# Moving the loads of the later layers' weights behind the first layer of the first group

## The chip, the core and the metric

The kernel runs on one core of a Trainium2 chip. The metric is the device time of one execution, in microseconds (us). A core has five engines with a queue of instructions each, worked off in order: TensorE (PE), VectorE (DVE), ScalarE (ACT), GpSimd (POOL) and SyncE (SP). Transfers are issued from the queues of SP, ACT and POOL; the issuing instruction stands in its queue like any other.

## What is computed

Four graph layers in a row, on 32 entries of 512 nodes with 256 features (float32), with one 512 x 512 matrix `adj` that is nearly all zeros: about eight entries a row besides the diagonal. Layers 0 and 3 are the same function with weights of their own (cut to what matters):

```python
pre_u = einsum('bud,dk->buk', h, W1[:d]);  pre_v = einsum('bvd,dk->bvk', h, W1[d:])
hidden = relu(pre_u[:, :, None, :] + pre_v[:, None, :, :] + b1)
S = sigmoid(einsum('buvk,ko->buvo', hidden, W2)[..., 0] + b2[0])
a = einsum('buv,bud->bvd', S * A, h)
m = einsum('uv,bud->bvd', A, h) * h
z = beta1 * h + beta2 * (a @ Wa + ba) + beta3 * (m @ Wm + bm)
```

Layer 1 is `z + relu((adj @ z) @ W.T + b)`, layer 2 an attention over all nodes with `W1`, `W2`, `b2`, `bias2` and `adj` added to the logits.

## The kernel before, in words

S is needed only where `adj` is not zero. The kernel counts the entries of a row first (class `Counts`) and branches: with few of them it takes `sparse_path`, which is what runs here. (`dense_path` is built as well and is not executed.)

**Tiles and groups.** The 32 entries are worked off in eight groups of four (`NB = 4`). For a group and a layer of the first kind there are these stages:

- `first`: the four entries are loaded (line 830, tile `h`), turned on PE (line 585), copied to `hT` by ACT (line 588) and put back to memory as `xT` (line 589). `pre` multiplies them with `W1` (line 601): the u half gets its bias on DVE (line 610) and is put into a table in memory (line 611, SP), the v half is copied by ACT (line 613, tile `v`) and put too (line 614, SP). DVE adds both for the diagonal (line 616) and sums them with `W2` (line 618). For each entry this is done in two halves of the nodes, so that a group has eight u and eight v puts. This needs of the weights only `W1`, `b1`, `W2` and `b2`.
- `edges`: 36 items of 128 table rows each are gathered (line 662, POOL, tile `rows`), the row of the other node is added (line 747, DVE; tile `mine`, loaded at line 708 by SP or gathered), and ReLU, `W2` and a sum follow (lines 755, 763 on DVE, line 733 on ACT). The results are put into a dense matrix in memory (line 655, POOL, `cells`). A gather may read any row, so the first one waits for all sixteen table puts.
- `middle`: the dense S is loaded back (line 791), and the rest of layer 0, layers 1 and 2 and the first stage of layer 3 follow, mostly on PE. Here `Wa`, `Wm` and the weights of layers 1 and 2 are used for the first time; for the first group `middle_before` makes some of it ahead.
- then `edges` again for layer 3, and `last`.

**The start.** Before all this, `Edges.build` makes the lists of the non-zero entries out of `adj`: four pieces that turn `adj` (lines 297 to 305), four that count along the rows and put `lists` into memory (lines 315 and 316), then for each eight positions a masked sum on DVE (line 359) and a Sign with a sum on ACT (line 370), and four gathers of `lists` (line 349, POOL). `zeros` writes zeros over the cells in memory, eight transfers of 512 KB from POOL (line 566).

**The other weights.** `Model.rest` is a generator with six pieces of code between its yields. Its first piece issues all loads of the weights that the first stage does not use: `gnn_loads` for layers 0 and 3 (three `beta`, line 84; `Wa` and `Wm`, line 120; `ba` and `bm` spread over the partitions, line 124: these on ACT's queue; `ba` and `bm` as columns, line 95, on SP's) and `others_loads` for layers 1 and 2 (`b2`, line 84, and the two weights at lines 147 and 148 on ACT; three columns on SP). That makes 17 loads on ACT and 7 on SP. The later pieces scale them by the betas on DVE (lines 131 to 138) and turn the weights of layers 1 and 2 on PE (line 160), copied by DVE (line 161). `ba`, `bm` and the two weights land in one buffer named `big` (2048 columns); the others have places of their own.

**What sets the order.** `sparse_path` gives each of these generators a list of times in units of a group, one per piece, and `weave` calls the pieces in the order of those times. That is the order in which the program is written down; a scheduling layer then places the instructions on the engines, and may move one ahead of others of its engine where nothing that it needs forbids that. In the built program all transfers that SP and ACT issue take one of eight semaphores in turn, and each waits until the last transfer on its semaphore has landed. The times that matter here: `setup` from -0.40 to -0.295, the `first` of group 0 from -0.385 to -0.30, `setup_behind` (the rest of `Edges.build`) from -0.285, `setup_rest` (the rest of `Model.rest`) from -0.26 to -0.20, and the edges of group 0 from -0.292.

Of the kernel before, what the change touches and what calls it, by code (L numbers as in the profile page):

```python
# [425 lines left out]
class Sparse:  # L426
# [110 lines left out]
    def setup(self):  # L537


        for w in (self.m.g0, self.m.g3):  # L540
            self.nc.vector.tensor_scalar(w["nb2"], w["b2"], -1.0, None, ALU.mult)
        self.zero = self.act.tile([P, GROUP], F32, name="zero", tag="hWa3")
        self.nc.gpsimd.memset(self.zero, 0.0)

        edges = self.built = self.e.build(self.counts, self.adjT, self.lists, self.psum, self.big, self.act)
        for _ in range(NC):
            next(edges)
            yield
        self.rest = self.m.rest(self.big(F32, 2048), self.psum)
        next(self.rest)  # L550
        self.zeros("0")
        yield
        for _ in range(NC + 2 * (OWN // 2 + 1)):
            next(edges)
            yield
# [609 lines left out]
def even(n):  # L1165
    return [1.0] * n
# [7 lines left out]
def spread(shares, a, b):  # L1174

    times, at = [], 0.0
    for share in shares:
        times.append(a + (b - a) * at / sum(shares))
        at += share
    return times  # L1180


def edge_times(ahead, a, b, behind, lead=LEAD):

    step = (b - a) / ITEMS
    first = [ahead + j * min(step, (a - ahead) / lead) for j in range(lead)]
    return first + spread(even(ITEMS), a, b) + spread(even(TAIL), b, behind)


def middle_shares(given):  # L1190


    hWa = [] if given else [1.7, 1.7]
    shares = list(hWa)
    for b in range(NB):
        more = hWa if b < NB - 1 else []
        shares += [] if given else [2.8, 2.8]
        shares += [3.4, 3.4, 1.0, 2.7]
        shares += [1.7, 3.4, 2.8, 4.5] + [0.9] * NC
        shares += [0.4, 0.4, 0.4, 1.0, 0.4, 1.0] + more + [1.5, 1.5]  # L1200
        shares += [2.8, 4.5] + [0.4] * NC + [0.5, 0.5]
    return shares + [0.1]


@with_exitstack
def sparse_path(ctx, m, counts, xr, outr, B):


    sp = Sparse(ctx, m, counts, xr, outr, B)
    last = B // NB - 1  # L1210
    streams = [
        (sp.setup(), spread(even(NC + 1 + NC + 2 * (OWN // 2 + 1) + 1), -0.40, -0.295), ""),
        (sp.setup_behind(), spread(even(2 * (OWN // 2 + 1) + 2 * PANELS + 4), -0.285, -0.16), ""),
        (sp.setup_rest(), spread(even(7), -0.26, -0.20), ""),
        (sp.zeros_behind(), spread(even(2), 0.15, 0.2), ""),
    ]
    for t in range(last + 1):
        g0, g3 = Group(sp, m.g0, f"0_{t}"), Group(sp, m.g3, f"3_{t}")
        start, end = (max(0.0, k - 0.47) for k in (t, t + 1))

        if t == 0:
            first = spread(FIRST, -0.385, -0.30)
            edges0 = edge_times(-0.292, -0.27, -0.03, -0.02, LEAD_AT_ENDS)
        elif t == 1:
            first = spread(FIRST, -0.28, -0.06)
            edges0 = edge_times(0.02, 0.07, start - 0.06, start - 0.04)
        else:
            first = spread(FIRST, start - 0.82, start - 0.56)
            if t > 2:
                first = [start - 1.25, start - 1.2] + spread(FIRST[2:], start - 1.14, start - 0.86)  # L1230
            edges0 = edge_times(start - 0.552, start - 0.505, start - 0.06, start - 0.04)
        edges3 = edge_times(end + 0.003, end + 0.05, end + 0.48, end + 0.54)
        parts = [(0, NB, end + 0.53, end + 0.56, end + 1.16)]
        if t + 3 <= last:
            parts = [(0, 2, end + 0.53, end + 0.56, end + 0.84), (2, NB, end + 1.06, end + 1.16, end + 1.46)]
        if t == last - 1:
            edges3 = edge_times(end + 0.003, end + 0.05, end + 0.46, end + 0.5)
            parts = [(0, NB, end + 0.67, end + 0.7, end + 1.06)]
        if t == last:
            end -= 0.2  # L1240
            edges3 = edge_times(end + 0.003, end + 0.02, end + 0.45, end + 0.46, LEAD_AT_ENDS)
            behind = end + 0.28, end + 0.4
        streams += [
            (sp.first(g0, t * NB), first, FIRST_US),
            (sp.edges(g0, ("yT", "mhT0", "hWa0") if t == 0 else ()), edges0, "free" if t > 2 else ""),
            (sp.middle(g0, g3, t * NB), spread(middle_shares(t == 0), start, end), "main"),
            (
                sp.edges(g3, *((("yT", "h1", "hT1"), ("mhT0", "hWa0")) if t == last else ())),
                edges3,
                "free",  # L1250
            ),
        ]
        if t == 0:
            streams.append((sp.middle_before(g0, 0), spread(AHEAD, -0.15, -0.03), ""))
        if t < last:
            for lo, hi, ahead, a, b in parts:
                times = [ahead] + spread(even((hi - lo) * 8 + 1), a, b)
                streams.append((sp.last(g3, t * NB, lo, hi), times, [0.0] + LAST_US * NB))
        else:
            streams.append((sp.last_before(g3, t * NB), spread(ENDS, *behind), ""))  # L1260
            streams.append((sp.last_half(g3), [end + 0.385] + spread(HALF_END, end + 0.42, end + 0.47), "free"))
            streams.append((sp.last_behind(g3, t * NB), spread(BEHIND, end + 0.5, end + 0.6), ""))
    sp.weave(streams)
# [191 lines left out]
@with_exitstack  # L1455
def adj_seq_kernel(ctx: ExitStack, tc: tile.TileContext, a: dict, out: bass.AP):
    nc = tc.nc
    x = a["x"]
    B = x.shape[0]
    xr = x.rearrange("b (c p) d -> b p c d", p=P)  # L1460
    outr = out.rearrange("b (c p) d -> b p c d", p=P)
    m = Model(ctx, tc, a)
    counts = Counts(ctx, m)
    excess = nc.values_load(counts.excess[0:1, 0:1])
    with tc.If(excess > 0) as branch:
        dense_path(m, xr, outr, B)
    with branch.Else():
        sparse_path(m, counts, xr, outr, B)
# [32 lines left out]
```

## Time and profile before

| | us |
|---|---|
| median of 3 runs | 2929.45 (2928.38 to 2934.63) |
| the profiled execution | 2945.73 |
| its span, first to last instruction | 2944.0 |

| engine | busy us | share | instructions |
|---|---|---|---|
| PE | 2679.6 | 91% | 9670 |
| DVE | 2294.8 | 78% | 5771 |
| POOL | 1565.7 | 53% | 1326 |
| ACT | 1319.1 | 45% | 3973 |

The profile divides the span into 40 slices of 73.6 us. PE's busy tenths in them begin 6, 3, 6, 7, 8, 8, 8 and are 8 or 9 nearly everywhere after that; the DMA engines moved 276, 294 and 255 GB/s in the first three slices. So the start is the part in which PE is least busy.

The start in order of time, from the timeline: `adj` has landed by 9.9 us and the branch is taken by 13.6; the load of the first entry goes at 13.63, the weight loads on ACT from 16.46 to 44.27, the zeroing transfers from 23.50 to 27.90; the first u is made at 29.88, the first v copied at 44.32; the last table put of the first group goes at 73.09 and its first gather at 81.20; DVE takes the first gathered rows at 88.34; the dense S is loaded from 208.86 on, and the first product with it (line 920) comes at 243.24.

How the views read: a timeline row is start, length, engine, line, operation, tile written <- tiles read. In brackets stands the idle time of the engine before it and what ended that. A "q" behind an engine's name means its queue, where a transfer is issued. In the list of waits a row is who waited <- for what, then us in total, how often, and the longest. The "chain that ended last" is followed back from the last instruction, at each step to what released it.

### The profile page before, as it was taken

The numbers are of one execution on the slowest core, as the hardware profiler recorded it, in microseconds if no ns is written. First come the engines' busy times: TensorE is split into PE (matmuls) and PEld (weight loads), VectorE is DVE, ScalarE is ACT, GpSimd is POOL, SyncE is SP. The second block draws the span as 40 slices with busy tenths as digits, with TensorE's granted clock in tenths as the row PEclk, the third lists the DMA queues.
The fourth block names the chain that finished last, engine by engine and source line by source line (L and its number), as shares of the span: only waits on it lengthen the run. The fifth ranks groups of instructions, "written<-read, shape, count | busy, mean of one in ns | idle before, by whom it ended". The sixth has DMA issues, their size and how long they took to land.

```text
span 2944.0 us, 33843 instructions
## 1 busy us (share of the span) xinstructions
PE 2679.6 (91%) x9670; PEld 1820.6 (62%) x9670; DVE 2294.8 (78%) x5771; ACT 1319.1 (45%) x3973; POOL 1565.7 (53%) x1326
## 2 busy tenths in 40 slices
PE   6367888989999998999899998999999999989998
PEld 5344445656666665666666676666666667655767
DVE  6884887979598885988778895989868896793494
ACT  3553454534354443545344443535435453453262
POOL 2671553746347572566537563575626664371173
PEclk9688889999999999999999999999999999999999
DMA  8874756886777878677786868777776875672474
GB/s 276 294 255 143 246 178 221 275 267 203 255 242 219 270 227 252 219 259 239 235 260 203 292 201 263 239 228 251 240 247 217 294 224 193 207 227 100 147 254 143
DMA packets 315457, 677.39 MB, mean 230 GB/s; under 512 B 53632, under 2 KB 188288, under 8 KB 307072
## 3 DMA queue, kind: packets, MB, share of 16 engines
q0 software_dynamic: 122400, 412.30, 43.8%
q1 hardware_dynamic: 161104, 225.62, 23.8%
q10 hardware_dynamic: 31760, 37.24, 3.6%
q8 instruction: 78, 1.28, 0.2%
q14 instruction: 115, 0.94, 0.1%
HBM read 529.02 MB, written 146.01 MB: 229 GB/s over the span
## 4 chain that ended last, share of the span: by engine, by line
PE 60%; DVE 20%; DMA 11%; issue 4%; ACT 3%; POOL 2%; SPq 0%; ACTq 0%; POOLq 0%; DVEq 0%
PE pst L46 28%; PE pst L601 9%; DVE rows L747 6%; PE pst L1100 6%; PE pst L920 5%; DVE rows L763 3%; DVE rows L755 3%; DMA rows<-table,iv 3%; PE pst L1112 3%; PE pst L927 2%; PE pst L941 2%; PE pst L963 2%; PE pst L1032 2%; DMA xT<-hT 1%; DMA table<-u 1%
## 5 line engine op out<-in xcount | busy, mean ns | idle before, releaser
L662 POOL DMA_INDIRECT rows<-table,iv x552 | 683.3, 1238 | 757.1 <-ACT rows L733 124.2
L655 POOL DMA_INDIRECT cells<-s,cell x576 | 714.6, 1241 | 383.9 <-DVE s L691 158.4
L747 DVE TENSOR_TENSOR rows<-rows,mine 128x1024 f32<-128x1024 f32 x551 | 665.5, 1218 | 125.1 <-DMA rows<-table,iv 71.8
L733 ACT ACTIVATE rows<-rows 128x256 f32<-128x256 f32 x1088 | 439.6, 406 | 505.4 <-DVE rows L755 456.0
L46 PE MATMUL pst<-adj,h 128*128 128x512 f32 x1024 | 454.5, 594 | 4.3 <-DMA h<-x2s 4.3
L763 DVE SCALAR_TENSOR_TENSOR rows<-rows,L_gnn_W2bc 128x256 f32<-128x256 f32 x1120 | 414.8, 419 | 2.7
L755 DVE SCALAR_TENSOR_TENSOR rows<-rows,L_gnn_W2bc 128x1024 f32<-128x1024 f32 x272 | 330.1, 1216 | 1.0
L46 PEld LDWEIGHTS pst<-adj,h 128*128 128x128 f32 x1024 | 192.8, 191 | 223.2 <-issue 219.3
L46 PE MATMUL pst<-L_gnn_Wa,hT 128*128 128x256 f32 x1024 | 252.2, 398 | 65.4 <-DMA hT<-xT 59.6
L601 PE MATMUL pst<-w_L_gnn_W,hT 128*128 128x256 f32 x1024 | 257.5, 404 | 30.5 <-ACT hT L588 18.2
L46 PEld LDWEIGHTS pst<-L_gnn_Wa,hT 128*128 128x128 f32 x1024 | 202.8, 202 | 103.6 <-issue 32.0
L601 PEld LDWEIGHTS pst<-w_L_gnn_W,hT 128*128 128x128 f32 x1024 | 204.9, 204 | 71.4 <-ACT hT L588 20.1
L46 PE MATMUL pst<-eT,feats 128*128 128x512 f32 x512 | 232.6, 608 | 11.4 <-ACT eT L1033 11.4
L601 PE MATMUL pst<-w_L_gnn_W,yT 128*128 128x256 f32 x1024 | 229.3, 382 | 5.7 <-DVE yT L1010 5.7
L46 PE MATMUL pst<-adjT,zW 128*128 128x512 f32 x512 | 225.6, 593 | 1.5 <-ACT zW L945 0.8
L601 PEld LDWEIGHTS pst<-w_L_gnn_W,yT 128*128 128x128 f32 x1024 | 196.0, 192 | 43.0 <-issue 8.1
L1100 PE MATMUL pst<-hWa,SA 128*128 128x256 f32 x896 | 219.6, 399 | 0.0
L1100 PEld LDWEIGHTS pst<-hWa,SA 128*128 128x128 f32 x896 | 214.1, 327 | 5.5 <-issue 2.6
L733 ACT ACTIVATION_READ_ACCUMULATOR rows<-rows 128x1 f32 x1088 | 204.6, 188 | 0.0
L920 PE MATMUL pst<-flat,hWa 128*128 128x512 f32 x448 | 196.8, 592 | 0.0
L889 ACT COPY flat<-SA 128x512 f32<-128x512 f32 x128 | 135.9, 1132 | 117.1 <-PE pst L46 99.9
L46 PEld LDWEIGHTS pst<-eT,feats 128*128 128x128 f32 x512 | 99.3, 196 | 127.6 <-issue 110.8
(179 smaller groups left out, 3669.2 us busy)
## 6 DMA issues: line engine op xcount, KB each, us to landing
SA<-cells POOLq DMA_DIRECT2D x62, 1024.0 KB
table<-u SPq DMA_DIRECT2D x128, 256.0 KB
table<-v SPq DMA_DIRECT2D x128, 256.0 KB
mine<-table SPq DMA_DIRECT2D x64, 512.0 KB
hT<-xT SPq DMA_DIRECT2D x36, 512.0 KB
h<-in_x_dram SPq DMA_DIRECT2D x64, 256.0 KB
xT<-hT ACTq DMA_DIRECT2D x64, 256.0 KB
h<-in_x_dram SPq DMA_DIRECT2D x32, 512.0 KB
```

The lines of the kernel that those rows point to most:

```text
L46: nc.tensor.matmul(out, lhsT, rhs, start=(n == 0), stop=(n == len(pairs) - 1))
L601: nc.tensor.matmul(p[:, k * D : (k + 1) * D], at(d, c + k), w["W1"][:, half * DC + d, :], start=(d + k == 0), stop=(d * k == 1),)
L655: ins = self.nc.gpsimd.indirect_dma_start(out=g.cells[half], out_offset=bass.IndirectOffsetOnAxis(ap=at, axis=0), in_=s, in_offset=None)
L662: self.nc.gpsimd.indirect_dma_start(out=rows, out_offset=None, in_=g.table, in_offset=bass.IndirectOffsetOnAxis(ap=at, axis=0))
L733: self.behind(nc.scalar.activation(part, part, AF.Identity, accum_out=g.s[:, k, b : b + 1]))
L747: self.behind(nc.vector.tensor_tensor(rows, rows, other, ALU.add))
L755: nc.vector.scalar_tensor_tensor(by_entry, by_entry, 0.0, w2, ALU.max, ALU.mult)
L763: nc.vector.scalar_tensor_tensor(part, part, 0.0, w["W2bc"], ALU.max, ALU.mult, accum_out=at)
L889: self.nc.scalar.copy(flat[:, r, :], SA[r][:, :, b])
L920: nc.tensor.matmul(pz, hWa[:, r, cs], flat[:, r, :], start=(r == 0), stop=False)
L1100: self.nc.tensor.matmul(pz[:, k * D : (k + 1) * D], SA[r][:, cs, b], hWa[:, r, :], start=(fresh and r + k == 0), stop=(end and k == 1 and ...
L1112: self.nc.tensor.matmul(pz[:, k * D : (k + 1) * D], mhT[:, d, cs], g.w["Wm"][:, d, :], start=(alone and d + k == 0), stop=(not alone and k ...
```

## The change

The call that ran the first piece of `Model.rest` inside `setup` is taken out. The stream `setup_rest`, which used to run the remaining pieces, now runs that first piece too, with a time of its own, -0.2995: behind the last piece of `first` of group 0 (about -0.304) and the last one of `setup` (about -0.300). Before, the loads were written down in the fifth piece of `setup`, at about -0.379.

```diff
@@ class Sparse, setup
             next(edges)
             yield
         self.rest = self.m.rest(self.big(F32, 2048), self.psum)
-        next(self.rest)
         self.zeros("0")
         yield
         for _ in range(NC + 2 * (OWN // 2 + 1)):
@@ sparse_path
     streams = [
         (sp.setup(), spread(even(NC + 1 + NC + 2 * (OWN // 2 + 1) + 1), -0.40, -0.295), ""),
         (sp.setup_behind(), spread(even(2 * (OWN // 2 + 1) + 2 * PANELS + 4), -0.285, -0.16), ""),
-        (sp.setup_rest(), spread(even(7), -0.26, -0.20), ""),
+        (sp.setup_rest(), [-0.2995] + spread(even(7), -0.26, -0.20), ""),
         (sp.zeros_behind(), spread(even(2), 0.15, 0.2), ""),
     ]
```

The buffer `big` is still taken in `setup`, at the same place. The number and the size of all transfers and the number of all instructions stay as they are. What the built program makes of it: PE's instructions have the same order as before. On ACT, the six loads into `big` (lines 124, 147, 148) stand around the fifth and sixth copy of v; the other eleven stand, as before, ahead of the first copy, between the copies of `adjT` and `hT`. On SP the seven column loads keep their places; of the later ones, the second load of `mine` stands ahead of the last v put of group 0. On POOL the second gather of `lists` stands ahead of the first four gathers of `rows`, and one later gather of `rows` behind four puts of `cells`. On DVE the scaling of the weights (lines 131 to 138) and the making of `iv` and `cell` stand differently among the work of the first stage; the order from the ninth item of the first edges on is the same.

## The prediction

> **What bounds the kernel now.** I read the page first: PE is busy for 91% of the span, and its weak slices are the first three and one near the end. The change touches only the start, so I went on to the chain that ended last, in order of time, for the first 100 us.
>
> ```profile
> span 2944.0 us, 33843 instructions
> ```
>
> ```profile
> 25.51 10.90 DMA h<-in_x_dram
> 36.43 0.39 ACTq L120
> 36.85 7.47 DMA big<-in_L_gnn_bm_dram
> 44.36 0.44 issue
> 44.80 0.60 ACT hT L588
> 45.44 3.78 PE pst L601 x8
> ...
> 83.74 9.34 DMA rows<-table,iv
> 93.10 1.23 DVE rows L747
> ```
>
> Columns: start, length, what. The load of h lands at 25.51 + 10.90 = 36.41, and at 36.43 ACT issues the load of Wm of layer 3 (line 120). A weight load had been standing at the head of ACT's queue until an earlier transfer landed, because in the built program every transfer of SP and ACT uses one of eight semaphores in turn and waits for the last user of its own. Behind the weight loads stands the copy to hT, which comes at 44.80 only. So the stall that the change aims at lies on the chain. How long it is, and who else stands still, is in the waits from 24 to 100 us (us in total, times, longest):
>
> ```profile
> ACT v L613 <- DMA big<-in_L_gnn_bm_dram: 18.5, 2, 17.0
> ```
>
> ```profile
> DVE rows L747 <- DMA rows<-table,iv: 8.3, 2, 7.4
> DVE pst L616 <- ACT v L613: 4.5, 2, 4.0
> DVE L_gnn_bcol L134 <- DMA bc_L_gnn_beta<-in_L_gnn_beta_dram: 3.8, 1, 3.8
> ```
>
> ACT loses 17.0 us, but DVE only 4.0 us to it; DVE had just lost 3.8 us to a weight's landing, and loses 7.4 us again before the first gathered rows. The windows say what limits in between (stretch, length, busy time of PE, PEld, DVE, ACT and POOL, granted PE clock, DMA share, GB/s):
>
> ```profile
> 32.00:36.00 4.00, 4.00 (x22) 3.07 (x21) 0.96 (x9) 0.00 (x0) 0.00 (x0) 1.00 1.06 405
> 36.00:40.00 4.00, 3.00 (x16) 2.13 (x14) 3.26 (x9) 0.00 (x0) 0.00 (x0) 1.00 1.05 408
> 40.00:44.00 4.00, 0.00 (x0) 0.00 (x0) 0.91 (x3) 0.00 (x0) 0.00 (x0) 1.00 0.98 327
> 44.00:48.00 4.00, 2.56 (x6) 2.11 (x7) 2.77 (x8) 2.19 (x5) 0.00 (x0) 0.55 1.06 380
> 56.00:60.00 4.00, 4.00 (x22) 3.54 (x21) 4.00 (x15) 3.56 (x10) 0.00 (x0) 1.00 1.02 327
> ...
> 60.00:77.00 17.00, 16.41 (x92) 14.28 (x91) 16.70 (x66) 13.23 (x33) 1.06 (x1) 1.00 0.80 262
> 77.00:90.00 13.00, 5.02 (x26) 3.93 (x24) 5.64 (x19) 1.17 (x2) 6.97 (x7) 0.69 1.02 354
> ```
>
> From 28 to 44 us the 16 DMA engines are full (the eight zeroing transfers of 512 KB are issued from 23.50 on); from 45 to 81 us DVE has no pause over 0.6 us (16.70 of 17.00). So an earlier start of this dense stretch is worth what DVE's pauses before it shrink, not the 17 us of ACT.
>
> **The change, part by part.** The instructions of PE keep their order; ACT, DVE, SP and POOL change theirs in the first 130 us. Of the 17 loads on ACT, 11 (betas, Wa, Wm, b2) still stand before the first copy v; so do the 7 columns on SP. Only six move behind: ba and bm of both layers (128 KB each) and the two 256 KB weights (lines 147, 148).
>
> (a) ACT's stall. Ahead of the first v there stood, from 26.74 on, seven loads (a xT put between them) that go at 26.74, 29.51, 30.95, 33.09, 36.43, 36.85 and 40.76, then the two of lines 147 and 148 at 43.37 and 43.79. In their place stand Wa, xT, Wm, b2, four issues that need no landing later than what the fourth issue of before (30.95, 1.29 long) needed: ACT comes free at about 32.2, and v follows when its product is there (31.06 + 1.89 = 32.95) instead of at 44.32. Next late: the third xT put, which waits for the second one's landing. That landing is 40.74 now, since b2's load, on the same semaphore, goes at 40.76; it may be 42 to 43 with Wa in front of it. So the second v and hT come near 44 instead of 47.60 and 48.08.
>
> (b) DVE. Its queue now has line 131 (Wa of layer 3) ahead of the first line 616, where line 134 stood, waiting for a beta until 36.74. Wa's load is issued near 26.8 behind the first xT put, 256 KB with 256 KB in front; call its landing T. Between two landings in this queue at that time, 36.7 (the beta) and 40.74 (xT), lie 4 us for one such 256 KB transfer. I take T = 38.5; ends 36.7 and 40.9. From T to the line 610 of the third u stand lines 131, 359, 616, 315, 618, 610, 618, 359, 315, 359, 359, 616, 359, 618. By start-to-start distances of those rows (0.55 for line 131, 0.67 for 359 and 315, 0.61 for 616 and 610, 0.34 for 618) that is 0.55 + 5 x 0.67 + 2 x 0.67 + 2 x 0.61 + 0.61 + 3 x 0.34 = 8.1 us. So the third u comes at 38.5 + 8.1 = 46.6, against 49.84: 3.2 us earlier. The late T leaves 49.84 - 40.9 - 8.1 = 0.8 us, the early one 5.0 us. DVE reaches the second line 616 at T + 6.5 = 45.0, and its v is there near 44.5 by (a), so that wait cuts the gain only where T is early. I take 3.2 (0.8 to 5.0). PE no longer pauses long enough to fall to 0.55 of its clock, which hides behind DVE.
>
> (c) Work put into or taken out of the dense stretch: lines 131 (Wa, 0.55) and 137 (0.13) leave it, 135 and 138 of layer 0 (0.26 and 0.39 at 77.11 and 77.90), which ran in a pause, enter. Zero, to 0.1. Six issues on ACT now stand between the fifth and the sixth v, 0.34 to 0.70 us each in their rows, some 2.7 us; three Sign rows of line 370 (0.9 us each) that stood there are done before, in the freed 33 to 44 us. So no price; if a semaphore is late there (the xT put behind them waits for the ba load's landing), the cover is gone and it costs up to 3 us. I take 0.5 (0 to 3).
>
> (d) The last table put. On SP the second load of mine (512 KB) moves in front of the last v put, and on POOL the second gather of lists (512 KB) in front of the four gathers of rows, which wait for that put.
>
> ```profile
> 71.27 0.33 SPq L708 DMA_DIRECT2D mine<-table  x1
> 71.69 0.39 SPq L611 DMA_DIRECT2D table<-u  x1
> 73.09 0.36 SPq L614 DMA_DIRECT2D table<-v  x1
> 73.50 0.47 SPq L708 DMA_DIRECT2D mine<-table  x1
> ```
>
> The first gather goes at 81.20, so SP's 512 + 256 + 256 KB took from 71.27 to 81.2: 1.05 MB in 9.9 us, 106 GB/s. At that rate 512 KB in front cost 4.9 us; at the 354 GB/s of all queues from 77 to 90, 1.5 us; nothing if the load uses the 1.4 us between the u and the v put and what competes now from 73.50. I take 2 (0 to 4.9), near the rate of all queues, as the same load competes with the put already. The second gather of lists costs POOL 1.25 us in a wait that is there anyway, and it takes as much off the gathers that follow.
>
> The Trainium skill (DMA: Bandwidth & Descriptors, Queues, rings and completion order) speaks against the change here: on each DMA engine a queue's descriptors are consumed in the order of its ring, and the queues that have work take turns. With three queues busy the load in front would get a third of 354 GB/s, an estimate of 4.4 us from that page; with 4.4 in place of 2 the sum below would be +0.7. The row does not decide between them.
>
> (e) DVE's pause before the first rows (7.36 us before 88.34) now holds lines 682, 395, 155 and 161 (twice, the second just behind the first 747) and 396, which ran in the dense stretch after 93: 0.09 + 0.10 + 0.07 + 0.33 + 0.33 + 0.12 = 1.0 us. I take -1.0 (-1.0 to 0). One gather of rows also moves behind four puts near 122, 6 us later; its reader is at 147.86, so it costs nothing, or up to 1 if transfers take 20 us.
>
> Sum: -3.2 + 0 + 0.5 + 2 - 1.0 = -1.7 us; the ends add to -6.0 and +8.2. After that the order is the same on all engines and the chain runs through edges and middle stages, so the shift stays. The profiled execution took 2945.73 (span 2944.0): with the change 2944.0. It lies 16.3 us over the median of the runs, 2929.45, so the shift is put on that: 2927.75, or 2927.5 in round numbers. About 0.2% (5.9 us) is what a measurement of this kernel can tell from no change, and this is within it.
>
> **Rivals.** *All of DVE's pauses go* (faster): Wa lands before 33, 3.8 + 4.0 us are won at the start, 1.0 in (e), and the load in front of the last put costs 1.5 only: -7.3 us, 2922. For it: PE's clock of 0.55 in 44 to 48 and its pause of 6.4 us vanish as well, and 1 MB of loads leaves the crowded 30 to 44 us. Against it: line 131 stands at the head of DVE, and DMA is at 1.05.
>
> *The last put is late* (slower): the load of mine takes its 4.9 us in front of it, the second gather of lists another 1.5 us of the full DMA engines and 1.5 in front of the rows on POOL's queue: 7.9, less the late end of (b), 0.8, and (e), 1.0: +6.1, 2935.5. It decides from the point where the put lands over 4 us later after its issue than now (8.1). For it: 1.02 of DMA from 77 to 90. Against it: the load's bytes are not new.
>
> *The change does not do what it says*: 11 of 17 loads stay early, and Wa, xT and Wm hold ACT until 43 as before: 2929.5, no change.
>
> **How the numbers follow.** Forecast 0.36, no effect 0.06: within 0.2%, 0.42 together. Faster by over 0.2%: 0.32; slower: 0.26. The time is the forecast's, 2927.5. The bounds of the sum give 2923.4 to 2937.6 and the faster rival 2922; the three runs of before lie up to 1 below and 5 above their median, so the range is 2919 to 2938; within the forecast alone 2924 to 2933.
>
> **What would show it.** The first line 613 near 33, not 44.32. DVE's pause before line 131 ending at T: later than 41 makes (b) wrong. Line 610 of the third u near 46.6. The first line 662 near 80: earlier than 77 means (d) is oversized, later than 82 undersized. The first line 747 near 87, the first line 920 near 241 instead of 243.2; if the shift there is not the shift of the end, the later stages do not simply follow, and the reasoning is wrong as a whole.

## The result and the profile after

| | before | after |
|---|---|---|
| median of 22 runs each, taken in turn (us) | 2933.91 (2923.68 to 2942.14) | 2939.53 (2931.46 to 2949.34) |
| the profiled execution, its span | 2945.73, 2944.0 | 2940.76, 2939.0 |
| mean granted PE clock in it | 0.957 | 0.959 |

The ratio after to before is 1.0021, with a 95% interval of 1.0012 to 1.0029. The change makes the kernel slower by 5.6 us by the medians, by 3.5 to 8.5 us by the interval. The forecast was 1.95 us faster, 2927.5 us. Of the 12.0 us between that and 2939.5, 4.5 lie in the starting point (the median of before was 2929.45 in three runs and is 2933.91 in 22), and 7.6 in the shift (5.6 + 1.95).

The profiled execution of after was 5 us shorter than that of before while the medians say the opposite, so the totals of two profiles decide nothing here. What they can show is where the work of the first 150 us moved.

```profile
span 2939.0 us, 33850 instructions
```

The chain that ended last, of after, from 24 to 130 us in order of time (start, length, what):

```profile
26.78 13.19 DMA L_gnn_Wa<-in_L_gnn_Wa_dram
...
54.80 4.87 DMA table<-v
59.69 6.17 DMA big<-in_L_gnn_W_dram
...
72.12 4.71 DMA table<-u
76.89 8.12 DMA mine<-table
85.06 0.95 POOL rows L661
...
92.57 11.40 DMA rows<-table,iv
```

From the removed line (550 of before) on, line numbers of after are one lower than those of before. The load of `bm` (36.85 to 44.32) has left the chain. In its place stand the landing of `Wa` at 39.97 (13.19 us after its issue), one of the moved loads at 59.69, the third load of `mine` at 76.89, and a gather of rows that takes 11.40 us. That the first gather at 85.06 waits for this load of `mine` is inferred from times alone (it lands at 85.01). By the semaphores in the trace the gather waits for the last v put, whose last part lands at 84.30; in all four profiles of after the gather follows that landing by 0.76 or 0.77 us.

The waits of after, 24 to 100 us (who, for what: us in total, times, longest):

```profile
DVE rows L746 <- DMA rows<-table,iv: 13.0, 3, 9.6
...
POOL rows L661 <- DMA mine<-table: 8.8, 1, 8.8
...
DVE L_gnn_Wa L131 <- DMA L_gnn_Wa<-in_L_gnn_Wa_dram: 6.7, 1, 6.7
...
ACT v L612 <- DMA table<-v: 3.9, 1, 3.9
```

ACT's wait of 18.5 us for the load of `bm` is gone. DVE's wait for gathered rows, 8.3 us before, is 13.0 us now: what the start wins is handed back there, and more.

The windows of after (stretch, length, busy time of PE, PEld, DVE, ACT, POOL, granted PE clock, DMA share, GB/s); the first four answer to stretches shown of before:

```profile
40.00:44.00 4.00, 1.44 (x4) 1.19 (x5) 4.00 (x11) 0.25 (x1) 0.00 (x0) 0.70 0.96 354
44.00:48.00 4.00, 4.00 (x11) 2.41 (x10) 4.00 (x13) 4.00 (x11) 0.00 (x0) 0.50 1.02 329
60.00:77.00 17.00, 15.30 (x87) 13.04 (x86) 15.96 (x61) 10.12 (x25) 2.08 (x2) 1.00 0.95 273
77.00:90.00 13.00, 5.84 (x23) 4.69 (x22) 3.62 (x17) 0.59 (x1) 3.79 (x4) 0.71 0.93 321
88.00:92.00 4.00, 4.00 (x12) 3.01 (x13) 1.78 (x4) 0.00 (x0) 3.08 (x4) 0.50 1.02 300
92.00:96.00 4.00, 2.98 (x13) 2.07 (x12) 1.55 (x2) 2.19 (x9) 3.09 (x4) 0.90 0.99 184
```

From 40 DVE works where it paused before (4.00 of 4.00 against 0.91). From 77 to 90 it does less than before (3.62 against 5.64). And from 92 to 96 the DMA engines are as full as ever (0.99) but move 184 GB/s. The same stretches of before:

```profile
92.00:96.00 4.00, 0.00 (x0) 0.00 (x0) 3.08 (x4) 1.29 (x7) 3.22 (x3) 0.50 1.04 418
96.00:100.00 4.00, 0.39 (x1) 0.39 (x2) 4.00 (x11) 3.72 (x20) 3.30 (x3) 0.50 1.03 409
```

Equally full engines moved 418 GB/s there. That drop is the main thing to explain.

### The profile page after: what moved, and what is told of

Its sections match the earlier page's. It is cut to its first block, busy times and chain, and to the rows that moved or that the text cites. A ratio compares the mean times of both kernels' runs of the same rounds, so it can differ in the third digit from the quotient of the medians.

```text
span 2939.0 us, 33850 instructions
## 1 busy us (share of the span) xinstructions
PE 2677.6 (91%) x9670; PEld 1818.0 (62%) x9670; DVE 2293.7 (78%) x5771; ACT 1319.4 (45%) x3973; POOL 1561.9 (53%) x1326
## 4 chain that ended last, share of the span: by engine, by line
PE 58%; DVE 23%; DMA 10%; issue 5%; ACT 2%; POOL 2%; ACTq 0%; SPq 0%; POOLq 0%; DVEq 0%
PE pst L46 27%; PE pst L600 8%; DVE rows L746 7%; PE pst L1099 6%; PE pst L919 5%; DVE rows L762 4%; DVE rows L754 3%; DMA rows<-table,iv 3%; PE pst L1111 3%; PE pst L926 2%; DMA table<-u 2%; PE pst L962 2%; PE pst L940 2%; PE pst L1031 1%; DVE pst L615 1%
```

## The experiments

Two measures are used. The *ratio* is time over that of before, from runs taken in turn on one chip (12 of the kernel unless said otherwise, 29 or 35 of before). The *mark* is where DVE starts the eleventh addition to a `rows` tile (147.86 us in before; the expectations call it the tenth add): from there to the end of that stage the order on the engines is that of before. In before, after and `diag_behind` (below) that row reads:

```profile
147.86 1.22 DVE L747 TENSOR_TENSOR rows<-rows,mine 128x1024 f32<-128x1024 f32 x1
```

```profile
151.39 1.22 DVE L746 TENSOR_TENSOR rows<-rows,mine 128x1024 f32<-128x1024 f32 x1
```

```profile
148.86 1.21 DVE L749 TENSOR_TENSOR rows<-rows,mine 128x1024 f32<-128x1024 f32 x1
```

DVE does not pause in front of it in any of the three. The table gives, for each kernel's own profile, the first gather of rows, the issue of the two diagonal puts `cells<-self_s` (line 686 of before), the mark, and the ratio.

| kernel | first gather | diagonal puts | mark | ratio (95%) |
|---|---|---|---|---|
| before | 81.20 | 97.84 | 147.86 | |
| before_again | 80.52 | 96.28 | 147.58 | 0.9988 (0.9973 to 1.0003) |
| after (22 runs) | 85.06 | 86.64 | 151.39 | 1.0021 (1.0012 to 1.0029) |
| after_again | 81.93 | 86.57 | 148.81 | 1.0022 (1.0003 to 1.0042) |
| after_third (profile only) | 82.86 | 86.71 | 151.87 | |
| after_fourth | 83.22 | 86.91 | 150.10 | 1.0013 (0.9994 to 1.0032) |
| mine_first | 80.87 | 85.03 | 148.13 | 0.9993 (0.9978 to 1.0008) |
| early_loads_again | 81.47 | 83.45 | 148.52 | 1.0007 (0.9995 to 1.0019) |
| put_first | 82.91 | 100.11 | 147.94 | 1.0023 (1.0005 to 1.0041) |
| put_first_again | 82.45 | 99.77 | 147.61 | 1.0011 (0.9993 to 1.0029) |
| loads_on_pool | 79.27 | 99.01 | 147.60 | 1.0009 (0.9994 to 1.0025) |
| rest_later | 83.37 | 100.04 | 147.87 | 0.9995 (0.9979 to 1.0011) |
| rest_later_again | 80.72 | 98.50 | 146.30 | 0.9994 (0.9980 to 1.0007) |
| loads_sooner | 80.28 | 99.25 | 147.07 | 1.0013 (0.9999 to 1.0027) |
| loads_latest | 80.40 | 84.87 | 149.33 | 1.0014 (0.9999 to 1.0029) |
| diag_behind | 85.28 | 99.75 | 148.86 | 1.0005 (0.9988 to 1.0023) |
| diag_behind_again | 83.44 | 99.09 | 147.85 | 1.0016 (1.0000 to 1.0031) |
| delay | 80.50 | 97.17 | 152.67 | 1.0029 (1.0011 to 1.0048) |

### How much two profiles and two series of one kernel differ

`before_again` is before, and `after_again`, `after_third` and `after_fourth` are after, without an edit.

> The unchanged kernel of before once more, for a second profile and for the scatter of the comparison. Ratio to before 1.000, interval about 0.0008 to either side. The marks of the start that the comparison of the two profiles rests on should come out again to within 0.5 us: first line 613 at 44.3, v of the eighth step at 72.5, first gather of rows at 81.2, first load of SA at 208.9. If the first gather moves by 2 us or more between two profiles of the same kernel, then the 3.9 us by which it is later in the changed kernel (85.06) is mostly scatter, and the start does not explain the result.

> The changed kernel once more, for a second profile. In five profiles (before twice, and three variants) the tenth add of line 747 of the first edges lies at 147.3 to 148.1 us wherever the first gather of rows lay (79.3 to 83.4); in the changed kernel at 151.4, with the first gather at 85.1. Theory (the loss is made between 73 and 104 us, in the transfers in front of and among the first gathers, and is of the kernel): the tenth add at 150 to 152 again, first gather at 84 to 86, ratio 1.001 to 1.003. Rival (scatter of one execution): tenth add within 0.7 us of 147.9, and the loss of the runs is made later.

> The changed kernel a third time, a profile alone, with the same marks: tenth add at 150 to 152 by the theory, 147.2 to 148.6 if the first profile was scatter.

> The changed kernel again, beside the next two on one chip, and a fourth profile of it. Tenth add at 148.8 to 152 as in the three before; time 4 to 8 us over before.

The marks of after lie at 148.81 to 151.87, mean 150.54; the two of before at 147.86 and 147.58, mean 147.72. So after stands 2.8 us later there (1.1 to 4.2 by the single profiles of after against the mean of before). One profile of after alone would have said 1 or 4. Later on the profiles of one kernel drift apart: at the first product with the dense S those of before stand at 243.24 and 242.19, those of after between 241.12 and 246.38 (mean 244.0), and the shift can't be followed from there in single executions.

The second profile of before also shows what an advance in the dense stretch is worth. Additions to `rows` on DVE in before_again:

```profile
87.57 1.23 DVE L747 TENSOR_TENSOR rows<-rows,mine 128x1024 f32<-128x1024 f32 x1 [3.89 <-DMA rows<-table,iv]
...
147.58 1.23 DVE L747 TENSOR_TENSOR rows<-rows,mine 128x1024 f32<-128x1024 f32 x1
```

Here the ninth u came at 78.62, 2.7 us later than in the first profile (75.96). DVE waited 3.89 us for rows instead of 7.36, and at the mark the two profiles of before are 0.28 us apart. In this pair, between about 73 and 100 us the transfers set the pace, and an advance or a delay of some 3 us on DVE before them is swallowed.

### The order on SP and POOL (d)

`mine_first` is before with after's order of the last table put: the second load of `mine` ahead of the eighth v put (an order without a wait). The scheduler then also placed the second gather of `lists` ahead of the rows, and the multiplication of the diagonal early on DVE, as in after. `early_loads_again` is the same kernel in another series. `put_first` is the reverse on after: the load held behind the put; the gather of `lists` and the multiplication went back with it.

```diff
 mine_first, on before:
+ins = nc.sync.dma_start(t, places[c, 0])
+if spare and c == 1:
+    self.tc.add_manual_dep(g.last_v.ins, ins.ins.name, order, reason="ahead of the last v")
 put_first, on after:
+if spare and c == 1 and not own_tags:
+    self.tc.add_manual_dep(ins.ins, g.last_v.ins.name, order, reason="behind the last v")
```

> Before, with one order on SP's queue turned round: the second load of mine (512 KB) in front of the eighth v put, as in the changed kernel; the weight loads stay where they were. Theory one (the load of mine in front of the last put costs what the changed kernel shows at the first gather): the eighth v put is issued at 73 as before, the first gather of rows comes near 85 instead of 81.2, the time is 3 to 6 us over before (1.001 to 1.002). Rival (the order on SP is harmless, the late weight loads crowd the DMA engines from 56 to 85 us): first gather within 1 us of 81.2, time within 2 us of before.

> Before with the second load of mine in front of the eighth v put once more (all weight loads early, the orders of the changed kernel on SP, POOL and DVE around the first gathers). Both theories: tenth add at 147.5 to 149, within 2.5 us of before. If it is 3 us or more over before with such a start, then neither the loads nor the start but scatter between kernels of this size is left.

> The change, with the second load of mine held behind the eighth v put on SP's queue by an order alone (no wait); in the built program the second gather of lists then stands behind the first four gathers of rows again, and the scaling by diag behind the first adds, all as before. The six loads stay at the fifth and sixth v. Theory (late loads and these moves together make the loss): first gather at 80 to 82.5, tenth add within 0.7 us of 147.9, time within 3 us of before. Rival (the late loads alone, by what they leave unsent in the DMA engines at 72 us): first gather at 84 or later, tenth add at 150 to 152, time 3 to 6 us over before.

> The changed kernel with the second load of mine behind the eighth v put, on another chip and beside the changed kernel: its start was that of before (147.9), its time was 5 us over it. Theory (the start decides, and that time was scatter): tenth add at 147.5 to 148.3, time within 2.5 us of before and 4 us or more under the changed kernel. Rival (late weight loads cost time somewhere behind the first edges): 4 us or more over before, level with the changed kernel.

With the load in front and the loads into `big` as early as in before, the first gather came at 80.87 and 81.47 against 81.20: the order alone costs nothing that can be seen, and the two ratios lie on both sides of 1. `put_first` brings the mark back to that of before (147.94 and 147.61), yet its ratios are 1.0023 and 1.0011. So a kernel whose profiles have lost nothing by the mark can still be about as slow as after. A part of the loss seems not to pass through the mark.

What makes the last put land later is where the six loads stand. From its issue to the first gather it takes 4.8 to 8.4 us (mean 6.9) in the six profiles with loads issued by 47 us, and 7.8 to 12.0 us (mean 9.9) in the twelve with loads issued from 52 us on; with late loads and the order of before (`put_first`) it is 10.0 and 10.4.

### When and from where the six loads go (c)

How the moved loads hold ACT shows in its timeline in after:

```profile
33.32 0.59 ACT L612 COPY v<-pst 128x512 f32<-128x512 f32 x1 [5.98 <-PE pst L600]
...
59.69 0.39 ACTq L147 DMA_DIRECT2D big<-in_L_gnn_W_dram  x1
60.12 0.59 ACT L587 COPY hT<-pst 128x512 f32<-128x512 f32 x1 [1.69 <-PE pst L584]
63.43 0.45 ACTq L148 DMA_DIRECT2D big<-in_L_gnn_W_dram  x1
63.97 0.54 ACTq L588 DMA_DIRECT2D xT<-hT  x1
64.62 0.59 ACT L612 COPY v<-pst 128x512 f32<-128x512 f32 x1 [3.92 <-DMA table<-v]
```

The load of line 148 is issued at 63.43 only: a put of a u on SP, issued at 57.53, holds the same semaphore until it lands at 63.41. Behind it stand an xT put and the copy to v, which ends an idle time of 3.92 us. Four kernels vary this; in `loads_on_pool` POOL, which is free, issues the loads at 31.78 to 37.97 us, so that they are early again.

```diff
 loads_on_pool, on after (the six loads into big):
-nc.scalar.dma_start(
+nc.gpsimd.dma_start(
 rest_later, loads_latest, loads_sooner, on after:
-[-0.2995] + spread(even(7), -0.26, -0.20)
+[-0.27] / [-0.26] / [-0.34]
```

> The change, with the six loads into big issued by POOL, which has nothing to do between 28 and 74 us, and not by ACT; the scheduler then leaves the eighth v put in front of the second load of mine, as before. Theory one (what was won at the start, 2 to 3 us, was lost because ACT stood still at those loads, and 3.9 us more to the load of mine): no ACT pause over 1.5 us between 45 and 70, v of the eighth step near 70, first gather of rows near 78.5, time 2 to 3 us under before (0.999). Rival (the bytes of the late loads in the crowded stretch cost it, whichever engine hands them out): first gather at 82 or later, time 3 to 6 us over before as the changed kernel.

> The change, with the first piece of the other weights at -0.27 instead of -0.2995: in the built program the six loads then stand around the sixth and seventh v (one later), and the eighth v put stands in front of the second load of mine again. Theory one: ACT stands still at the loads as in the changed kernel, so nothing is won in the dense stretch (eighth v near 71 to 73), but the first gather of rows comes at 81 to 82; time within 2 us of before. Rival (late weight loads crowd the DMA engines): first gather near 85, time 4 to 6 us over before.

> The changed kernel with the first piece of the other weights at -0.27: loads around the sixth and seventh v, late, but a start as before (tenth add at 147.9 in its first profile, time level with before). Theory one (late loads cost some 4 us behind the first edges): 3 to 6 us over before. Theory two (only the start counts, about 1.2 us for each us of it): tenth add at 147.5 to 148.5 and within 2.5 us of before.

> The first piece of the other weights at -0.34: the six loads stand together behind the fourth v, the two loads of mine one after the other in front of the eighth u and v. Theory one (late loads cost some 4 us): 3 to 6 us over before. Theory two (the start counts): its tenth add at 147.9 plus x, and 1.2 x over before, within 2.5 us; with two loads of mine in front of the last puts I expect x of 1 to 3.

> The first piece at -0.26: the six loads stand around the sixth and seventh v and the last one behind the seventh, the orders on SP and POOL are those of the changed kernel, with the diagonal puts early. Theory one (late loads): 3 to 6 us over before, whatever the start mark. Theory two (the start counts): tenth add 1 to 4 us late as in the changed kernel, and 1.2 times as much over before.

`rest_later` was not quite what its expectation says. The second load of `mine` still stood in front of the last v put (72.17 and 72.72 us), only the gather of `lists` went behind the rows and the diagonal's multiplication came late again. Read so, it says more: with the load in front and a first gather 2.2 us later than in before, the mark is 147.87 (146.30 in the second series) and both ratios are just under 1. A gather that starts 2 us late is swallowed as well. And the theory that late loads cost about 4 us by themselves falls, since `rest_later` has its loads late too. `loads_on_pool`, without the hold on ACT, has the earliest first gather of all (79.27) and gains nothing by it, at the mark or at the end. It can't tell the hold on ACT from the late bytes, since both are gone, and its ratio is no clean comparison: its loads no longer take their turn at the eight semaphores, so that 611 of SP's 629 transfers carry another one than in before, to the end. `loads_sooner` has both loads of `mine` in front of the last puts and a mark of 147.07; its ratio, 1.0013, decides between neither of its theories. What separates the marks in the table is the column of the diagonal puts: the seven profiles with early puts (83 to 87 us) have marks from 148.13 up, mean 149.74; the ten with late ones, leaving out `delay`, have 146.30 to 148.86, mean 147.65. The ranges overlap, and the early puts cost little by themselves: with early loads (`mine_first`, `early_loads_again`) the marks are 0.4 and 0.8 us over the mean of before.

### The diagonal puts (e)

SP's timeline, of before and of after:

```profile
97.84 0.89 SPq L686 DMA_DIRECT2D cells<-self_s  x2
```

```profile
72.56 0.46 SPq L707 DMA_DIRECT2D mine<-table  x1
73.11 0.82 SPq L613 DMA_DIRECT2D table<-v  x1
...
86.64 0.89 SPq L685 DMA_DIRECT2D cells<-self_s  x2
```

Line 682 multiplies `self_s` by the diagonal on DVE, and the two puts at line 686 take what it writes. Each carries 4 KB, as 256 rows of 16 bytes that go to 256 places. In after the multiplication runs in DVE's pause, and so the puts go 11 us earlier, among the first gathers of rows. `diag_behind` holds the multiplication behind the fourth addition:

```diff
+adds.append(added.ins.name)
...
-nc.vector.tensor_tensor(g.self_s, g.self_s, diag, ALU.mult)
+ins = nc.vector.tensor_tensor(g.self_s, g.self_s, diag, ALU.mult)
+if spare and not own_tags:
+    self.tc.add_manual_dep(ins.ins, adds[3], order, reason="behind the fourth item")
```

This brings the puts back to 99.75 us. The scheduler then also moved a few later instructions: on DVE those around the fifth addition, two puts of the next group on SP, and the gather of rows behind four puts of `cells` on POOL, which stands where it did in before. That last move is not what counts: `put_first`, `rest_later` and `loads_sooner` have that gather late, as after has, and yet the marks of before.

> The change, with the multiplication by diag held behind the fourth add of rows on DVE, where it stood before, so that the two diagonal puts into cells (over a thousand packets of 16 bytes) go out near 100 us and not at 86.6 among the first gathers of rows. The second load of mine and the second gather of lists stay in front. Theory (the small packets among the first gathers make the loss: DMA moved 184 GB/s from 92 to 96 us at a share of 0.99): first gather still at 84 to 86, but the tenth add at 148 to 149, time within 3 us of before. Rival (the late last put makes the loss): tenth add at 150 to 152, time 3 to 6 us over before.

> The changed kernel with the multiplication by diag behind the fourth add, on another chip and beside the changed kernel. Theory (the small packets of the diagonal puts among the first gathers of rows are the loss): tenth add at 147.9 to 149, time 0 to 3 us over before, 3 us or more under the changed kernel. Rival (the first profile and time were scatter): tenth add at 149 to 152, time 4 to 8 us over before.

Where the first of these texts counts over a thousand packets it is wrong; the trace has 512 of 16 bytes for both puts. Windows and DVE timeline of `diag_behind` (line 749 is the addition), beside the window of `loads_latest` (early puts):

```profile
92.00:96.00 4.00, 3.15 (x14) 2.10 (x12) 3.46 (x4) 2.19 (x9) 3.09 (x4) 0.90 1.03 407
96.00:100.00 4.00, 0.00 (x0) 0.00 (x0) 4.00 (x7) 2.60 (x13) 3.39 (x3) 0.95 1.04 411
```

```profile
95.00 1.23 DVE L749 TENSOR_TENSOR rows<-rows,mine 128x1024 f32<-128x1024 f32 x1 [0.54 <-DMA rows<-table,iv]
...
101.48 1.23 DVE L749 TENSOR_TENSOR rows<-rows,mine 128x1024 f32<-128x1024 f32 x1 [0.53 <-DMA rows<-table,iv]
```

```profile
96.00:100.00 4.00, 0.00 (x0) 0.00 (x0) 2.00 (x4) 3.65 (x19) 1.28 (x2) 0.79 0.92 197
```

In `diag_behind`, with late puts, the stretch from 92 to 100 moves 407 and 411 GB/s, as in before, though the first gather is as late as in after (85.28). With early ones, one stretch between 92 and 104 falls to 184 (after), 253 (`after_again`), 232 (`after_third`), 221 (`early_loads_again`) or 197 (`loads_latest`), at a share of 0.92 to 1.04, and a gather's rows come late; in `after_fourth` and `mine_first` the lowest is 303 and 302. The two kinds do not overlap: of the stretches 92 to 96 and 96 to 100 the slower one moves 184 to 341 GB/s in all seven profiles with early puts and 353 to 417 in all eleven with late ones, `delay` included. Nor do DVE's pauses: ahead of the additions to `rows` behind the first, up to 115 us, it stands still for 2.5 to 4.9 us with early puts and for 0 to 1.7 us with late ones. For two profiles of after, the last additions on DVE before its long run of other work, after_again first and after_third below:

```profile
101.09 1.22 DVE L746 TENSOR_TENSOR rows<-rows,mine 128x1024 f32<-128x1024 f32 x1 [2.23 <-DMA rows<-table,iv]
```

```profile
104.52 1.22 DVE L746 TENSOR_TENSOR rows<-rows,mine 128x1024 f32<-128x1024 f32 x1 [4.47 <-DMA rows<-table,iv]
```

The marks of the two `diag_behind` profiles average 148.36, 2.2 us under the 150.54 of after: most of the 2.8 us by which after is late there comes from these two puts, in a kernel whose loads are late as well. The figure is rough, two profiles against four, and the single ones touch (148.86 and 148.81). In time the kernel lies at 1.0005 and 1.0016, between before and after; that these 2.2 us reach the end is not resolved by 24 runs. So the drop in rate goes with the place of the puts. How they cause it stays open. It is not the time that their packets take: in the trace of after each of the 512 takes 9 ns, 4.6 us in all, or 0.3 us on each of 16 engines. What fills the engines from 92 to 96 us there is the gathers themselves. Of 148 gather packets of 4 KB that start in it 37 take over 0.4 us, up to 2.0 us; in before there are 373, and none takes over 0.17 us. Such long packets also stand at 84 to 90 us in before, when no 16-byte packet is under way, and in `rest_later_again` 500 of the 512 go between 102 and 104 us without a long one beside them. The Trainium skill (DMA: Bandwidth & Descriptors, Specifications) says that below 512 bytes a transfer falls under the line rate, and that the engine then reads, modifies and writes. The rate agrees, 16 bytes in 9 ns against 4096 in 159 ns, but it does not account for the loss.

### Whether a shift at the mark stays to the end

`delay` is before with six fills of `zero` (0.91 us each) on DVE behind the sixth addition.

```diff
+if spare and not own_tags and k == 5:
+    for _ in range(6):
+        ins = nc.vector.memset(self.zero, 0.0)
+        self.tc.add_manual_dep(ins.ins, added.ins.name, order, reason="behind the sixth add")
```

> Before, with six more fills of the tile zero by DVE (0.91 us each where the kernel has one) behind the sixth add of line 747, so that the first edges come 5.5 us later from there on and nothing else is changed. Theory (a shift of the first edges goes to the end as it is): tenth add at 153.3 instead of 147.9, time 5 to 6 us over before, so the changed kernel's mean shift of 2.8 us at that mark is worth some 3 us and the rest of its 6 us is from elsewhere. Rival one (what is late there grows on the way): 9 us or more. Rival two (the edges have slack, and later stages take it up): under 2 us, and then the start of the changed kernel explains nothing.

The mark moved by 4.8 us (152.67), and the ratio is 1.0029: 8.5 us on 2934, with 3.2 to 14 us by the interval. A shift of this size at the mark is not wholly won back later.

## Why the prediction was wrong, step by step

**(a) ACT's stall: right.** The first v at 33.32 (forecast 33), the second at 44.47 (44).

**(b) DVE's start: right.** `Wa` landed later than thought. DVE's timeline of after:

```profile
39.99 0.49 DVE L131 TENSOR_SCALAR L_gnn_Wa<-L_gnn_Wa,bc_L_gnn_beta 128x512 f32<-128x512 f32 x1 [6.69 <-DMA L_gnn_Wa<-in_L_gnn_Wa_dram]
...
47.91 0.69 DVE L609 TENSOR_TENSOR u<-pst,bc_L_gnn_b 128x512 f32<-128x512 f32 x1
...
90.22 1.23 DVE L746 TENSOR_TENSOR rows<-rows,mine 128x1024 f32<-128x1024 f32 x1 [9.60 <-DMA rows<-table,iv]
...
95.43 1.23 DVE L746 TENSOR_TENSOR rows<-rows,mine 128x1024 f32<-128x1024 f32 x1 [2.45 <-DMA rows<-table,iv]
```

T was 39.99, inside the bounds of 36.7 to 40.9 and 1.5 us over the value taken, and the third u came at 47.91 instead of 46.6. So 1.9 us were won by then, 2.6 us by the sixth u (59.86 against 62.42). Over all profiles, four of after against two of before, the means give 3.2 us at the third u, the forecast's own figure, and 4.1 us at the sixth. PE's clock did not keep up, as the forecast thought it would: it was granted 0.50 from 44 to 48 us (0.55 before); as supposed there, that hides behind DVE, which has 4.00 of 4.00.

**(c) The six issues on ACT: the size was off.** Forecast 0.5 (0 to 3). Of the 2.6 us at the sixth u, 0.7 are left at the ninth (75.27 against 75.96): 1.9 us lost; by the means over all profiles 1.2 of 4.1 are left, 2.9 us lost, at the upper bound. The late semaphore that was named as a possibility came, on the load of line 148, with a u put of SP as its cause rather than the load of `ba`.

But (b) and (c) together should have reached the end, and they do not: `before_again` is 2.7 us later at the ninth u and level at the mark. The forecast took an earlier DVE in the dense stretch for an earlier end of it; from 73 to 100 us the rows' transfers come last, and they do not start the earlier for it. Here a first step failed: of the -2.7 us that (b) and (c) were to bring, nothing shows at the mark.

**(d) The last put: the size came out by luck, its cause and its effect were wrong.** From the issue of the last v put to the first gather, before took 8.1 us (73.09 to 81.20) and `before_again` 4.8. After took 11.95, 9.3, 8.5 and 10.3 in its four profiles, mean 10.0: 1.9 us more than the first profile of before, forecast 2 (0 to 4.9), and 3.6 more than both on average. But the load of `mine` in front is not the cause: with the order alone changed it took 8.4 and 7.6 (`mine_first`, `early_loads_again`), and with the order of before put back into after 10.0 and 10.4 (`put_first`). The delay goes with the late loads into `big`, to which the forecast gave no price here. The 4.4 us that the prediction worked out from the Trainium skill (DMA: Bandwidth & Descriptors, Queues, rings and completion order) are not seen either. And a gather 2 us later costs nothing at the mark (`rest_later`, `put_first`).

**(e) DVE's pause before the first rows: the main step that failed.** The forecast was -1.0 us (-1.0 to 0), from the durations of six DVE instructions that move into the pause. One of them is line 682, 0.09 us long, and the two puts that wait for it were not priced. They go at 86.6 us instead of 97.8, and DVE's waits for rows behind the first addition grow. What the runs put in place of the -1.0 is +2.2 us at the mark (after against `diag_behind`): a miss of 3.2 us, and outside the bounds, because they excluded a loss. In the terms of the sum, of the 4.5 us between -1.7 and +2.8 at the mark, 3.2 lie here, 2.7 in the advance of (b) and (c) that does not arrive, and -2.0 in the delay of (d) that does not arrive either; 0.6 are left over.

**The shift stays: right as far as it was tried** (`delay`). But the sum at the mark, -1.7 forecast and +2.8 measured, explains only half of the 5.6 us.

**The other half stays open.** `put_first` has before's mark and still 1.0023 and 1.0011; `rest_later` has it too and 0.9995 and 0.9994. Beyond 180 us the order of the instructions on every engine is the same in all, and so are the semaphores that they take, but for `loads_on_pool`. Put together over the runs of the experiments by least squares, with a level of its own for each series, after stands 4.8 us over before, `put_first` 3.9, `diag_behind` 2.7, `mine_first` (with `early_loads_again`) 1.3 and `rest_later` -0.4, each with a standard error of 1.3 us; `loads_sooner` and `loads_latest` stand at 3.0 and `loads_on_pool` at 5.2, with 1.7 to 1.8. So three kernels whose marks are those of before stand 3 to 5 us over it and a fourth, `rest_later`, does not. That is too coarse to tell whether some of these builds lose time in a later place; no profile showed such a place, since single executions wander more than that after 243 us.

**The rivals.** *All of DVE's pauses go* fell with `Wa`'s landing at 39.97. *It does not do what it says* fell with the first v at 33.32. *The last put is late* gave +6.1 us and came nearest in time (2935.5), but by luck and not by its mechanism: its condition, a landing over 4 us later after the issue than the 8.1 us of before, was met in none of the four profiles (3.8 at most), and a gather 2 us late alone costs nothing.

## What to carry to other kernels

When an instruction moves into an engine's idle time, price what it releases, not its own length: here 0.09 us of DVE sent two puts of tiny rows among gathers that were the bottleneck, and the gathers' rate fell. An advance counts only where the work that gains it ends last at the next meeting point; a second profile of the unchanged kernel, whose engines drift by some us, shows for nothing which stretches swallow such drifts. For a change of 0.2%, take the starting point from many runs and a mark from several profiles, because three runs and one profile each missed by 4 us or 2 us here.

## What the runs showed that was not expected

DMA engines that are full can move less than half as much: 184 GB/s at a share of 0.99 in after against 418 at 1.04 in before, in the same four microseconds. A transfer issue on ACT can be held by a put of another queue, since they share a semaphore in turn: 3.92 us of idle ACT in front of the sixth v. Two puts of 4 KB whose packets take 0.3 us of the 16 engines go along with gather packets of up to 2.0 us in place of 0.16. And with the spread between single runs of one kernel goes the mean granted PE clock: over all runs that list their clock, 0.001 of it goes with 2.6 us of time, where runs of one kernel have a standard deviation of 5.3 us.
